# Interleaving three passes of a windowed transformer in larger pieces, normalising P before it is turned, and multiplying with the values as the stationary operand

## The chip, the core and the metric

The kernel runs on one core of one Trainium2 chip. A core has five engines that work side by side, each through its own queue of instructions in order: TensorE (PE; its weight loads are listed as PEld), VectorE (DVE), ScalarE (ACT), GpSimd (POOL) and SyncE (SP), which issues most of the DMA transfers. PE reads two operands from SBUF, a stationary one that is loaded into the array and a moving one that is streamed through it, and writes its results to PSUM. The metric is the time of one execution on the device in microseconds (us), the median of the runs.

## The reference, cut to what matters

The model has four layers, each the product of a mixing branch and a gating branch. Two of the gating branches are complete transformers over the tokens: the first of six layers, 16 heads of 64 and a window of 32; the second of two layers, 8 heads of 64 and a window of 64. Each of their layers computes, for x of 4 x 512 tokens by 128:

```python
qkv = shift(x) @ Wqkv                       # q, k, v by heads of 64
q, k = rotary(l2norm(q) * qs), rotary(l2norm(k) * ks)
sim  = q . k                                # per window: own and previous block of keys
attn = softmax(where(mask, -max, 8 * sim))  # over 2 * window keys
x    = x + concat_heads(attn @ v) @ Wo
x    = x + ((xn @ W1a + b) * gelu(xn @ W1g + b)) @ W2 + b2   # xn: layer norm of shift(x)
```

The change touches these two transformers alone. All of it is in float32, apart from the additive mask, which is bfloat16.

## The kernel before

The kernel computes the layers one after the other. The two transformers (`transformer`, line 707, and the class `_Transformer`, line 1171) fill the stretches from about 1580 to 3410 us and from about 3480 to 3940 us of the profiled execution.

A transformer is run by three passes, which are Python generators: `queries_keys` (line 1268) makes q and k, `attention` (line 1476) everything from the scores to the residual, `feed_forward` (line 1523) the rest. A row is one layer of one of the four sequences of 512 tokens, and a slot is a row's group of eight heads: 6 x 4 rows of two groups are 48 slots in the first transformer, 2 x 4 rows of one group are 8 in the second. In each slot `merge` runs the three passes beside each other, each some slots behind the one before it: a pass gives up control with `yield cost`, and the pass that has done the smallest share of its total (10.3 for queries and keys, `attention_weight`, `feed_forward_weights`) goes on. So these costs decide in which order the products of the three passes stand in PE's queue. The framework puts the instructions of each engine into its queue when the program is built, and an engine works through it in order, waiting on semaphores.

The attention pass works in units: in the first transformer a unit is four heads (of a group's eight) over all 512 tokens, in the second four heads over 256 tokens. There are 96 units in the first (two per slot) and 32 in the second (four per slot). With i the unit at hand, the pass does in each step:

- `scores` (line 1370): two products with the mask and 64 small products (16 in the second) of q and k into one PSUM tile; each has 64 rows of the array and 32 columns (64 in the second). DVE takes the maximum (L1399), subtracts it into P (L1403, two instructions), ACT takes the exponential in place (L1408), DVE sums the rows (L1410) and inverts the sums into r (L1412). In the middle of the products stands the turn of unit i-1.
- `turn` (line 1415): eight transposes of P of unit i-1 by PE (L126, operands `core` and `l_P`), and ACT's copy PT (L1424).
- `turn_back` (line 1465) of unit i-2: its weighted values On, which have the tokens on the partitions, are transposed by PE (L126, `core` and `l_On`; eight transposes, four in the second transformer) and copied by ACT into OT (L1474, two instructions). If it is the second unit of a pair, four products with `Wo` (operands `l_OT` and `l_wo`, 512 columns, 256 in the second) and DVE's addition to the residual (L1513) follow.
- `weigh` (line 1427) of unit i-1: 64 products (16 in the second) in which PT is stationary and the values move; the values are `vo`, where two neighbouring blocks share the partitions, or `ve`, where the pairs begin one block earlier. DVE multiplies the result by r into On (L1454, two instructions of 128x512; in the second transformer one such instruction).
- `values` (line 1331): v of a later unit, copied by ACT into `vo`, and from there by SP's DMAs into `ve`.

A float32 product stands in the trace as two matmul records, each with its own weight load; a transpose is one record. All PSUM tiles come from one ring of four (`S2`), each two banks. POOL adds the squares (L1294) and the halves of the rotation (L1298) of q and k, four of each in a slot. DVE multiplies q and k with the tables (L1295, L1297) and with the inverse lengths (L1321), which come from the products with operands `sqp` and `l_k`. SP issues the DMAs that put q and k into the layout of the scores (`l_qk`, 16 in a slot), those of `ve` and the weights.

Of the kernel before, what the change touches and what calls it, by code (L numbers as in the profile page):

```python
# [16 lines left out]
F32 = mybir.dt.float32  # L17
# [1153 lines left out]
class _Transformer:  # L1171
    def __init__(self, net, pre, heads, window, pools, consts):
# [26 lines left out]
        self.attention_weight = 20.4 if self.split else 25.0  # L1199
# [22 lines left out]
    def part(self, kind, l, gp):  # L1222

        key = kind, l, gp
        if key not in self.weights:
# [8 lines left out]
            else:  # L1234
                t = self.WT.tile([128, 4, 128], F32, name=pre + "_wo", bufs=3)
                nc.sync.dma_start(t, a[pre + "Wo"][l][512 * gp : 512 * (gp + 1)].rearrange("(t p) n -> p t n", p=128))
# [31 lines left out]
    def queries_keys(self, rows):  # L1268
# [3 lines left out]
        for l, b in rows:  # L1272
# [4 lines left out]
            for gp in range(self.GP):  # L1277
# [3 lines left out]
                for i in range(2):  # L1281
# [3 lines left out]
                    for g in range(2):  # L1285
                        p = self.S2()
                        for h in range(2):
# [3 lines left out]
                            yield 0.86  # L1291
# [16 lines left out]
    def unit_length(self, sums, t):  # L1308
# [5 lines left out]
        for g in range(2):  # L1314
            net.mm(p[:, g, :], self.ones, sums[g][:, 0, :])
            yield 0.86
# [14 lines left out]
    def values(self, u):  # L1331
# [8 lines left out]
        for u0 in range(0, n, step):  # L1340
            p = self.S2()
            pv = p.rearrange("p a (b c) -> p (a b) c", c=1024 // self.NB)
            for k in range(u0, u0 + step):
                if self.split:
                    for e in range(2):
                        net.mm(pv[64 * e : 64 * e + 64, k - u0, :], hb[:, 64 * k : 64 * k + 64], w[:, 256 * e : 256 * e + 256])
                    yield 0.45
                else:
                    c = 128 * (n * tp + k)
                    net.mm(pv[:, k - u0, :], hb[:, c : c + 128], w)  # L1350
                    yield 0.86
# [18 lines left out]
    def scores(self, qk, tp, j, last):  # L1370
# [7 lines left out]
        for t in range(T):  # L1378
            if last and t == T // 2:
                yield from self.turn(last)  # L1380
            for g in range(2):
# [13 lines left out]
                yield 0.31  # L1395
        n = 4 * T
# [16 lines left out]
        return P, r  # L1413
# [13 lines left out]
    def weigh(self, u):  # L1427

        net, nc, W, T = self.net, self.nc, self.W, self.T
        PT, r, vo, ve, tp, j = (u[k] for k in ("PT", "r", "vo", "ve", "tp", "j"))  # L1430
        On = self.PP.tile([128, 2 * T, 2, 64], F32, name=self.pre + "_On", bufs=1)
        o = self.S2() if self.split else self.M()
        for i in range(2 * T):
            g = i % 2
            for bl in range(self.NB):
                c = self.NB * (T * tp + i // 2) + bl
                v, k = (vo if c % 2 else ve), c // 2 - tp * self.NU
                for e in range(2):
                    if self.split:
                        rows, d = slice(64 * e, 64 * e + 64), 64 * (2 * g + j)  # L1440
                        net.mm(
                            o[W * bl : W * bl + W, e, 64 * i : 64 * i + 64], PT[rows, i, W * bl : W * bl + W],
                            v[rows, k, d : d + 64],
                        )
                    else:
                        n, d = 2 * i + e, 64 * (4 * g + 2 * j + e)
                        net.mm(
                            o[W * bl : W * bl + W, 64 * n : 64 * n + 64], PT[:, n, W * bl : W * bl + W], v[:, k, d : d + 64]
                        )
            yield 0.3 if self.split else 0.15  # L1450
        rv = r.rearrange("p (n e) -> p n e", e=2)
        if self.split:
            for e in range(2):
                nc.vector.tensor_tensor(  # L1454
                    On[:, :, e, :], o[:, e, :].rearrange("p (n d) -> p n d", d=64),
# [251 lines left out]
```

## Time and profile before

| | |
|---|---|
| three runs | 3961.78, 3963.43 (median) and 3975.84 us |
| the profiled execution | 3955.01 us, of which the span from first to last instruction is 3953.3 us |
| PE | 3577.5 us busy, 90% of the span |
| DVE | 2452.6 us, 62% |
| ACT | 1845.0 us, 47% |
| POOL | 1157.9 us, 29% |
| granted TensorE clock | 0.942 of full speed on the mean of the span |

Busy time is the time in which at least one instruction of the engine is under way. Matmuls overlap, and the mean duration of one record is longer than the distance between the starts of two of them, so that a busy PE is not a PE at its peak. A group of instructions is one source line with one operation, its tiles (output, then inputs, buffer numbers left out) and its shape; most matmuls have the line of the helper that issues them, L122, and transposes L126, so that they are told apart by their tiles. For a matmul, 64*32 is the part of the array that it uses (rows by columns), and 64x64 the moving operand (rows by columns).

### The profile page before, as it was taken

What the parts mean: (1) busy time and instruction counts of PE and PEld (TensorE: products, weight loads), DVE (VectorE), ACT (ScalarE), POOL (GpSimd) and SP (SyncE); (2) the same over time, 40 slices, a digit from 0 to 9 for tenths busy, and PEclk for the clock granted to TensorE, in tenths of its full rate; (3) what the DMA queues carried; (4) which work ended last, traced back from release to release, by engine and by line L of the source; (5) the groups of instructions that cost most, each with busy time, mean ns of one, the idle gap of its engine ahead of it and who ended that gap; (6) DMA issues with size and microseconds to landing.
All of it is one profiled execution on the core that took longest, in us unless ns stands there. A gap on an engine that the chain in (4) does not pass through costs nothing.

```text
span 3953.3 us, 105287 instructions
## 1 busy us (share of the span) xinstructions
PE 3577.5 (90%) x46763; PEld 1880.3 (48%) x46891; DVE 2452.6 (62%) x3429; ACT 1845.0 (47%) x2510; POOL 1157.9 (29%) x994
## 2 busy tenths in 40 slices
PE   7786999899999998889999999999999999778887
PEld 4553455444444443444444554554444445445554
DVE  6674555413353341677777787777777777457774
ACT  3343666523133324454555554555455455535555
POOL 1000444300021112533334343343443343033220
PEclk7677999999699999999999999999999999889998
DMA  1000000001000001434344434334334333413221
GB/s 38 8 26 28 1 1 1 30 0 51 2 1 3 3 1 37 106 86 115 88 96 110 98 91 109 95 91 119 93 83 117 86 80 94 130 37 83 54 56 42
DMA packets 123574, 236.12 MB, mean 60 GB/s; under 512 B 29624, under 2 KB 44128, under 8 KB 117728
## 3 DMA queue, kind: packets, MB, share of 16 engines
q1 hardware_dynamic: 114064, 209.58, 21.7%
q10 hardware_dynamic: 8624, 19.29, 1.5%
q8 instruction: 369, 6.05, 0.6%
q0 software_dynamic: 432, 0.51, 0.1%
q14 instruction: 85, 0.70, 0.1%
HBM read 50.08 MB, written 5.54 MB: 14 GB/s over the span
## 4 chain that ended last, share of the span: by engine, by line
PE 62%; DVE 13%; ACT 12%; issue 6%; DMA 3%; POOL 2%; SPq 1%; DVEq 0%; ACTq 0%; POOLq 0%
PE S L122 39%; PE S L126 5%; PE M L122 5%; PE S L1389 4%; PE o L1094 3%; ACT l_P L581 3%; PE o L614 2%; DVE l_rot L1295 2%; DVE rotp L1297 1%; DMA l_tab<-in_k_rot_l 1%; DVE l_rot L1321 1%; PE S L1008 1%; ACT sqp L1293 1%; ACT l_PT L1424 1%; SPq L1328 1%
## 5 line engine op out<-in xcount | busy, mean ns | idle before, releaser
L1298 POOL TENSOR_TENSOR l_rot<-l_rot,rotp 128x1024 f32<-128x1024 f32 x224 | 528.6, 2362 | 324.7 <-DVE rotp L1297 313.3
L1294 POOL TENSOR_TENSOR sqp<-sqp 128x512 f32<-128x512 f32 x224 | 291.5, 1301 | 956.6 <-ACT sqp L1293 952.0
L122 PE MATMUL S<-hb,l_wqk 128*128 128x512 f32 x896 | 476.8, 622 | 38.1 <-ACT l_PT L1424 10.7
L1293 ACT ACTIVATE sqp<-S 128x1024 f32<-128x1024 f32 x224 | 230.2, 1027 | 305.1 <-PE S L122 304.1
L1321 DVE SCALAR_TENSOR_TENSOR l_rot<-S,l_rot 128x1024 f32<-128x1024 f32 x224 | 264.6, 1219 | 133.8 <-ACT S L1318 110.6
L126 PE MATMUL S<-core,l_P 128*128 128x128 f32 x1856 | 266.9, 288 | 40.1 <-ACT l_P L1408 17.3
L122 PE MATMUL S<-l_KT,l_QT 32*128 32x256 f32 (+7 forms) x1536 | 264.2, 510 | 34.7 <-ACT l_P L1116 14.5
L1295 DVE TENSOR_TENSOR l_rot<-S,l_tab 128x1024 f32<-128x1024 f32 x224 | 271.2, 1211 | 24.6 <-ACT sqp L1293 24.0
L1389 PEld LDWEIGHTS S<-l_qk 64*32 64x32 f32 (+1 forms) x13312 | 178.5, 108 | 217.7 <-issue 211.2
L1116 ACT ACTIVATE l_P<-S 128x1024 f32<-128x1024 f32 x160 | 156.7, 1022 | 252.3 <-PE S L122 251.7
L126 PEld LDWEIGHTS S<-core,l_P 128*128 128x128 f32 x1856 | 213.3, 146 | 128.1 <-issue 39.3
L1297 DVE TENSOR_TENSOR rotp<-S,l_tab 128x1024 f32<-128x1024 f32 x224 | 270.8, 1209 | 1.4 <-POOL l_rot L1298 1.3
L1389 PE MATMUL S<-l_qk 64*32 64x64 f32 (+1 forms) x13312 | 249.5, 230 | 18.8 <-DMA l_qk<-l_rot 1.7
L122 PE MATMUL S<-sqp,l_k 128*128 128x512 f32 x448 | 251.9, 648 | 13.4 <-POOL sqp L1294 6.6
L122 PE MATMUL S<-l_wv,hb 128*64 128x256 f32 (+1 forms) x1600 | 237.2, 400 | 5.5 <-DVE rotp L1297 4.2
L1069 DVE TENSOR_REDUCE l_mx<-S 128x2 f32<-128x768 f32 (+1 forms) x192 | 155.0, 864 | 136.7 <-PE S L1008 136.7
L122 PEld LDWEIGHTS S<-l_ve,l_PT 64*32 64x32 f32 (+1 forms) x6656 | 164.3, 108 | 152.5 <-issue 124.9
L1399 DVE TENSOR_REDUCE mx<-S 128x16 f32<-128x1024 f32 (+1 forms) x128 | 156.3, 1221 | 116.1 <-PE S L1389 112.2
L122 PEld LDWEIGHTS S<-hb,l_wqk 128*128 128x128 f32 x896 | 147.2, 191 | 168.6 <-issue 92.0
L122 PE MATMUL S<-l_OT,l_wo 128*128 128x512 f32 (+1 forms) x512 | 218.9, 543 | 8.3 <-DVE ffu L1551 7.9
L1120 POOL TENSOR_SCALAR_AFFINE_SELECT l_P<-l_P 128x256 f32<-128x256 f32 x256 | 99.4, 406 | 417.0 <-ACT l_P L1116 411.6
L1317 ACT ACTIVATE S<-S,l_tiny 128x1024 f32<-128x1024 f32 x112 | 121.9, 1089 | 198.4 <-PE S L122 180.2
(358 smaller groups left out, 6580.1 us busy)
## 6 DMA issues: line engine op xcount, KB each, us to landing
l_qk<-l_rot SPq DMA_DIRECT2D x896, 128.0 KB
l_ve<-l_vo SPq DMA_DIRECT2D x112, 256.0 KB
l_ve<-l_vo SPq DMA_DIRECT2D x96, 224.0 KB
l_tab<-in_k_rot_l ACTq DMA_DIRECT2D x16, 1024.0 KB
l_wqk<-in_l2Wqkv SPq DMA_DIRECT2D x12, 512.0 KB
l_wv<-in_l2Wqkv SPq DMA_DIRECT2D x12, 256.0 KB
l_wo<-in_l2Wo SPq DMA_DIRECT2D x12, 256.0 KB
l_ve<-l_vo SPq DMA_DIRECT2D x24, 128.0 KB
```

What stands on the lines that cost most here:

```text
L122: self.nc.tensor.matmul(out, lhsT, rhs, start=start, stop=stop)
L126: self.nc.tensor.transpose(out, in_, self.ident[:n, :n])
L1069: nc.vector.tensor_reduce(mxv[:, bs, 2 * m + e, 3 - i], s[u][:, :, c : c + n], axis=AX.X, op=ALU.max)
L1116: nc.scalar.activation(P[u], s[u], AF.Exp, scale=scale)
L1293: nc.scalar.activation(sq, p, AF.Square)
L1294: nc.gpsimd.tensor_tensor(sq[:, 0, :], sq[:, 0, :], sq[:, 1, :], ALU.add)
L1295: nc.vector.tensor_tensor(t[:, g], p, tab[:, 0], ALU.mult)
L1297: nc.vector.tensor_tensor(m, p, tab[:, 1], ALU.mult)
L1298: nc.gpsimd.tensor_tensor(t[:, g], t[:, g], m[:, ::-1, :], ALU.add)
L1321: nc.vector.scalar_tensor_tensor(t[:, g], p[:, g, :].unsqueeze(1).to_broadcast([128, 2, S]), 1e12, t[:, g], ALU.min, ALU.mult)
L1389: net.nc.tensor.matmul(sv[W * bl : W * bl + W, e, t, g, :].rearrange("p (s k) -> p s k", s=2), qk[0][r, g, j, W * c : W * c + W], kw, star ...
L1399: nc.vector.tensor_reduce(mx, flat, axis=AX.X, op=ALU.max)
```

## The change

Five things are edited, all in the two transformers.

1. The weighted values. In `weigh` the values become the stationary operand (64 rows and 64 columns of the array in the first transformer, 128 and 64 in the second) and PT the moving one, of 32 columns (64 in the second). The number of products stays at 64 (16). The result has the head's dimension on the partitions, which is what `Wo` needs: `turn_back` goes, with its transposes, and ACT copies the result into OT with two instructions of 128x512 (one in the second transformer, where there were two of 128x256).
2. The normalisation. As the tokens are no longer on the partitions after `weigh`, P itself is multiplied by r before it is turned, by one POOL instruction of 128x1024 per unit. DVE's multiplications L1454 go.
3. In the first transformer the blocks of even and odd number lie in different halves of PSUM and of the partitions, so that `Wo` is loaded a second time with its two halves of 64 rows exchanged (two more DMAs per load, two buffers of twice the size in place of three), and the product with `Wo` is eight products of 256 columns in place of four of 512.
4. The turn of unit i-1 stands behind all the scores of unit i in place of the middle of them.
5. A pass gives up control less often: after two products of q or k, after both sums of squares, after a whole PSUM tile of values, after half a unit of scores, after half a unit of `weigh`, after two products with `Wo`. The costs are those of the pieces together, and `attention_weight` is 18.6 and 23.0 in place of 20.4 and 25.0.

```diff
-        self.attention_weight = 20.4 if self.split else 25.0
+        self.attention_weight = 18.6 if self.split else 23.0
...
-                t = self.WT.tile([128, 4, 128], F32, name=pre + "_wo", bufs=3)
-                nc.sync.dma_start(t, a[pre + "Wo"][l][512 * gp : 512 * (gp + 1)].rearrange("(t p) n -> p t n", p=128))
+                t = self.WT.tile([128, 2 if self.split else 1, 4, 128], F32, name=pre + "_wo", bufs=2)
+                wo = a[pre + "Wo"][l][512 * gp : 512 * (gp + 1)].rearrange("(t p) n -> p t n", p=128)
+                nc.sync.dma_start(t[:, 0], wo)
+                if self.split:
+                    nc.sync.dma_start(t[0:64, 1], wo[64:128])
+                    nc.sync.dma_start(t[64:128, 1], wo[0:64])
...
                             net.mm(o.rearrange("p (s u k) -> p s u k", s=2, k=W) if i else o, w[:, c : c + 128], hk if i else hb)
-                            yield 0.86
+                        yield 1.72
...
             net.mm(p[:, g, :], self.ones, sums[g][:, 0, :])
-            yield 0.86
+        yield 1.72
...
                         net.mm(pv[64 * e : 64 * e + 64, k - u0, :], hb[:, 64 * k : 64 * k + 64], w[:, 256 * e : 256 * e + 256])
-                    yield 0.45
...
-                    yield 0.86
+            yield 1.8 if self.split else 1.72
...
         for t in range(T):
-            if last and t == T // 2:
-                yield from self.turn(last)
             for g in range(2):
...
-                yield 0.31
+            if t % 2:
+                yield 1.24
...
-        return P, r
+        Pn = P.rearrange("p t g e k -> p (t g e) k")
+        nc.gpsimd.tensor_tensor(Pn, Pn, r.unsqueeze(2).to_broadcast([128, n, 2 * W]), ALU.mult)
+        if last:
+            yield from self.turn(last)
+        return P
...
-                        net.mm(
-                            o[W * bl : W * bl + W, e, 64 * i : 64 * i + 64], PT[rows, i, W * bl : W * bl + W],
-                            v[rows, k, d : d + 64],
-                        )
+                        rows, d, s = slice(64 * e, 64 * e + 64), 64 * (2 * g + j), bl % 2
+                        x = 64 * (e ^ s)
+                        net.mm(ov[x : x + 64, s, i, bl // 2, :], v[rows, k, d : d + 64], PT[rows, i, W * bl : W * bl + W])
...
-            yield 0.3 if self.split else 0.15
-        rv = r.rearrange("p (n e) -> p n e", e=2)
-        if self.split:
-            for e in range(2):
-                nc.vector.tensor_tensor(
-                    On[:, :, e, :], o[:, e, :].rearrange("p (n d) -> p n d", d=64),
-                    rv[:, :, e].unsqueeze(2).to_broadcast([128, 2 * T, 64]), ALU.mult,
-                )
...
-    def turn_back(self, u, OT):
...
-        for i in range(2 * T):
-            net.transpose(t[:, i, :], u["On"][:, i].rearrange("p e d -> p (e d)"))
...
-        for g in range(2):
-            self.nc.scalar.copy(ov[:, u["j"], g], tv[:, g])
+            if i % T == T - 1:
+                yield 1.2 if self.split else 0.3
+        for s in range(2 if self.split else 1):
+            n = 2 * W
+            src = (o[:, s, :] if self.split else o).rearrange("p (t g q) -> p g t q", g=2, q=n)
+            dst = OT[:, s].rearrange("p (g j) (t q) -> p j g t q", j=2, q=n)
+            nc.scalar.copy(dst[:, j], src)
...
-                    for t in range(4):
-                        net.mm(p, wo[:, t, :], OT[:, t, :], t == 0, t == 3)
-                        yield 0.86 if self.split else 0.43
+                    parities = 2 if self.split else 1
+                    pv = p.rearrange("p (x s q) -> p s x q", s=parities, q=W)
+                    for s in range(parities):
+                        for t in range(4):
+                            net.mm(pv[:, s], wo[:, s, t, :], OT[:, s, t, :].rearrange("p (x q) -> p x q", q=W), t == 0, t == 3)
+                            if t % 2:
+                                yield 0.86
```

## The prediction

> **What bounds the kernel now.** I read the busy time by stage first, then the groups, then who waits for whom, then the chain in order of time. The page's totals (PE 90%, DVE 62%) mix stages; by stage (columns: busy time and instructions of PE, PEld, DVE, ACT, POOL, then clock, DMA share, GB/s), the first transformer's steady stretch and the second transformer are:
>
> ```profile
> 1690.00:3390.00 1700.00, 1623.06 (x28182) 843.14 (x28272) 1312.26 (x1452) 867.55 (x988) 650.54 (x398) 1.00 0.40 97
> 3560.00:3954.00 394.00, 337.29 (x2693) 192.30 (x2718) 262.85 (x336) 216.60 (x267) 95.09 (x66) 0.96 0.24 58
> ```
>
> PE is busy for 95% of the first and 86% of the second, DVE for 77% and 67%, POOL for 38% and 24%. The first is bound by PE, the second partly by chains. PE's waits in the first stretch (total, times, longest) are small, and the largest is for an instruction that the change removes:
>
> ```profile
> PE S L122 <- DVE l_On L1454: 18.3, 16, 1.4
> PE S L122 <- ACT l_PT L1424: 14.3, 33, 0.8
> PE S L122 <- DVE rotp L1297: 10.3, 11, 2.0
> PE S L122 <- ACT l_OT L1474: 9.2, 24, 1.3
> ```
>
> What PE's time consists of is seen in the chain in order of time (start, us, what):
>
> ```profile
> 2206.40 0.34 PE S L1389 x16
> 2206.74 1.06 PE S L122 x2
> 2207.80 0.66 PE S L1389 x45
> 2208.45 1.02 PE S L126 x8
> 2209.48 0.67 PE S L1389 x46
> ...
> 2220.94 3.63 PE S L122 x8
> ```
>
> The scores' 64*32 records come in bursts cut by 512-column products and transposes. A burst of 16 takes 0.34 us and one of 46 0.67: 0.011 us a record and 0.16 for the burst. Uncut bursts of 128 run to the next product's start in 1.41 us, so I take 0.010 a record and 0.18 a burst. Eight 512-column records take 3.63 and two alone 1.06, so 0.43 each and 0.20 for the run. Values bursts (128*64) cost 0.15 beside 0.108 a record, from their lengths 4 (0.58) and 12 (1.45). **Every change of the array's division costs PE 0.15 to 0.20 us.**
>
> **The change part by part.** PE is the bound, so its sum comes first.
>
> *Transposes of On*: 96 x 8 + 32 x 4 = 896 go. At (1.02 - 0.20) / 8 = 0.103 us each: -92 us. (Bounds: 0.103 and the group's 100.9 us for 728, 0.139.)
>
> *Fewer cuts.* In the order in which the built program has PE's products, runs with the whole array fall from 605 to 312 in the first transformer, bursts with 32 or 64 columns at 64 rows from 514 to 308, values bursts from 183 to 95; in the second from 105 to 68, 63 to 35 and 42 to 32. First: 293 x 0.20 + 206 x 0.18 + 88 x 0.15 = 109; second: 7 + 5 + 2 = 14. Together -123 us. (The removed transposes' runs are in this count.)
>
> *The weighted sum* keeps 12,288 records in the first transformer. Now each loads 32 columns and streams 64, in eight tiles of the array; after it loads 64 and streams 32, in four. In the second transformer it keeps its shape. No record of before is 64*64 with 32 streamed. The nearest rows are the second transformer's scores (64*64, 128 streamed) and its weighted sum (128*64, 64 streamed), start and duration in us:
>
> ```profile
> 3852.44 0.43 PEld L1389 LDWEIGHTS S<-l_qk 64*64 64x64 f32 x16 [0.42 <-issue]
> 3852.45 0.67 PE L1389 MATMUL S<-l_qk 64*64 64x128 f32 x16
> ...
> 3757.98 0.22 PE L122 MATMUL S<-l_ve,l_PT 128*64 128x64 f32 x1
> 3758.03 0.22 PE L122 MATMUL S<-l_vo,l_PT 128*64 128x64 f32 x1
> 3758.04 0.22 PE L122 MATMUL S<-l_ve,l_PT 128*64 128x64 f32 x1
> 3758.09 0.22 PE L122 MATMUL S<-l_vo,l_PT 128*64 128x64 f32 x1
> 3758.10 0.22 PE L122 MATMUL S<-l_ve,l_PT 128*64 128x64 f32 x1
> ```
>
> One half of the array takes a new 64-column weight every 0.058 us (3757.98, 3758.04, 3758.10). Among the 16 loads of the scores the first four, on four different tiles, start within 0.02 us and the next four 0.055 later, so four tiles load side by side: 0.058 / 4 = 0.0146 us a record. Ends: 0.010 if loads stay hidden (0), 0.0267 if the scores' own pace of 16 in 0.43 us is the loads' (+205 us). I take 0.0146, since the first loads show four at once: 12,288 x 0.0046 = **+57 us**.
>
> [...]
>
> *The product with Wo*: 48 x 8 records of 512 columns become 48 x 16 of 256, the same streaming; the second transformer's 256-column group runs at 22.3 us for 83, 0.27 overlapped, against 0.43 for 512, so between 0 and 48 x 16 x 0.05 = 38 us. Consecutive ones start 0.215 apart, half of 0.43: 0.
>
> PE's work: -92 - 123 + 57 = **-158 us**.
>
> *Waits that go*: DVE l_On -18 and ACT l_OT -9; in the second transformer transposes of On waited 8: **-35 us**. DVE loses 2 x 0.667 per unit, ACT's copies stay; neither was the bound: 0.
>
> *The wait that comes.* PT is copied by ACT (1.02 us) and `weigh` needs it. Before, half the scores, On's transposes and Wo stood between the transposes of P and `weigh` (every unit of the first transformer but two had over 1 us of PE work there); after, in PE's order, 48 of 96 units and 15 of 32 in the second have nothing between. From the last transpose's start to the copy's end before it is 1.32 us at best, 1.69 at the third quarter, 2.44 at the ninth tenth (behind another ACT instruction); PE loses some 1.4 after the 0.11 of streaming. 63 x 1.4 = **+88 us**. What is queued behind: all of PE, so this is paid in full. Ends: 1.2 (+76) and 2.3 (+145).
>
> *P on POOL.* L595 does the same in another layer: 128x1024 in 1.89 us. 128 of them, 242 us, on a POOL that is 38% busy; in the first transformer its share becomes about 50%. In POOL's queue it stands among the rotations (2.36) and sums (1.30); behind it wait the sums that PE's `sqp` products need. PE's cover for those is 2.9 us at the lowest quarter against 2.5 to 3.6 measured from product to sum: +5, ends 0 and 48 x 1.9 = 91. The chain of P grows: r is ready 7.2 us after the scores (middle value), P then some 11; the next scores end 19.4 later. Smallest slack in the first transformer 1.4 us: 0. In the second, units are 8 to 10 us apart and 1.3 to 3.4 short in half of them, 28 us in all, in place of 17 for which its turns waited on P: +15, ends 0 and 28.
>
> *SP*: 24 more DMAs at 0.6 us issue, and Wo's tile now waits for its last use but one; `l_qk` and `ve` queue behind. The chain holds 2.85 us of `l_wo` landing once. 12 loads: ends 0 and 35, I take 0, as q and k are made a slot ahead.
>
> *DVE under POOL*: the copies of `hb` take 0.42 us alone and 1.8 beside POOL; 14% more overlap on 2 per slot is 20 us of a DVE with 23% idle: 0.
>
> Sum: -158 - 35 + 88 + 5 + 15 = **-85 us** on the profiled 3955: 3870. The median of the runs lies 8.4 above the profile: **3878 us**, -2.1%.
>
> **Rivals.**
> *A, the waits stay hidden*: other waits shrink as PE pauses for PT. -158 - 35 = -193: 3770. For it: PE's present waits are 3.5% of the stretch. Against: nothing stands between in PE's order.
> *B, the loads are the bound* (slower): the 64*64 weight loads go two at a time, 0.0267 a record, +205 in place of +57: 3878 + 148 = 4026. It decides from 85 / 12,288 = 0.0069 above 0.0146, at 0.0215 us a record. For it: the scores' 16 loads in 0.43 us; against: the four simultaneous starts.
> *C, the gain goes into waits*: the copy comes at 2.4 us for all 63 units (+57) and POOL's queue delays P or the sums by a rotation (2.36) in a quarter of 128 units (+30 with the slack): 3965, no change. For it: PE's time per unit shrinks by 1 us while the chain grows by 4.
>
> **How the numbers follow.** Forecast (3810 to 3930) 0.55; A (3740 to 3810) 0.2; C (3930 to 3990) 0.13; B (above 3990) 0.12. The median of three runs tells about 0.5%, 20 us, from no change. Faster is the first two and a third of C: 0.8; same 0.08; slower B: 0.12. The range leaves out half of A's best and most of B: 3780 to 3985.
>
> **What would show it.** No l_On group; the weighted sum as 64*64 64x32 with bursts of 64 records at 0.0146 each, near 1.1 us; whole-array runs of two 512-column records rarer; PE waiting on ACT l_PT some 60 times over 1 us; POOL's new group at 1.89 us. Wrong if such a burst takes 1.7 us or more (B), or PE's busy share in the first transformer falls under 90% (C).

## The result: 0.6% slower, and the profile after

The changed kernel takes 3992.9 us on the median (six runs, 3986.8 to 3996.6) against 3965.6 us (six runs, 3960.3 to 3981.9): a ratio of 1.0056, with a 95% interval of 1.004 to 1.0072 (estimated over the runs, and not the quotient of the two medians). The forecast was 3878. The profiled execution took 3996.6 us, its span 3994.8.

Busy time by stage, the first and the second transformer (length, then busy time and instructions of PE, PEld, DVE, ACT and POOL, the clock, DMA share, GB/s). The stretches run from a transformer's first product with `l_wqk` to its last with `ffu`, the kernel before first:

```profile
1582.00:3425.00 1843.00, 1740.07 (x29808) 901.80 (x29902) 1403.37 (x1554) 938.97 (x1066) 711.42 (x435) 1.00 0.40 97
3496.00:3947.00 451.00, 387.98 (x3026) 218.57 (x3056) 309.08 (x389) 243.74 (x297) 125.75 (x84) 0.95 0.25 59
```
```profile
1592.00:3438.00 1846.00, 1667.25 (x29520) 986.44 (x29520) 1325.41 (x1363) 942.42 (x1066) 898.15 (x531) 0.97 0.40 99
3515.00:3988.00 473.00, 372.14 (x2928) 213.55 (x2927) 292.29 (x353) 241.13 (x262) 183.25 (x113) 0.90 0.23 56
```

PE is busy for 73 us less in the first and 16 less in the second, and yet the stages are 3 and 22 us longer. So PE stands idle for longer (length less busy time: 103 to 179 us and 63 to 101 us), and its mean clock fell from 1.00 to 0.97 and from 0.95 to 0.90.

The waits of PE in the first transformer, after (total, times, longest), and then the two longest in the second. The last three rows are the kernel before, l_rot and ffu in the first transformer and P in the second:

```profile
PE S L122 <- ACT l_PT L1431: 61.7, 63, 1.8
PE S L122 <- DMA l_wqk<-in_l2Wqkv: 25.0, 2, 14.0
PE S L122 <- DVE l_rot L1326: 23.1, 11, 4.9
PE S L122 <- DVE ffu L1544: 17.6, 18, 1.0
PE S L126 <- DVE rotp L1302: 13.6, 8, 4.6
...
PE S L126 <- POOL l_P L1417: 55.7, 12, 8.4
PE S L122 <- ACT l_PT L1431: 18.3, 16, 1.5
...
PE S L122 <- DVE l_rot L1321: 12.7, 8, 3.0
PE S L122 <- DVE ffu L1551: 2.7, 1, 2.7
PE S L126 <- ACT l_P L1408: 17.3, 10, 5.4
```

The waits for l_On are gone. Those for l_PT, 80 us in both stages, are the wait that was forecast (before, they were 17.5 us). Three others grew beyond the forecast: the weights of queries and keys (25 us in two waits, none before), l_rot and ffu (41 us; 15 before), and P in the second transformer (55.7 us; 17.3 before).

**The half clock.** PE in order of time around one new pause (start, us, instruction, and in brackets the idle time before it):

```profile
2497.73 2.74 PE L122 MATMUL S<-ffu,l_w 128*128 128x512 f32 x6
2500.31 1.04 PE L126 MATMUL S<-core,l_P 128*128 128x128 f32 x8
2503.11 0.25 PE L122 MATMUL S<-l_PT,l_ve 64*64 64x32 f32 x2 [1.76 <-ACT l_PT L1431]
...
2504.52 3.25 PE L122 MATMUL S<-sqp,l_k 128*128 128x512 f32 x4
...
2507.70 0.25 PE L122 MATMUL S<-l_PT,l_ve 64*64 64x32 f32 x2
...
2508.77 1.52 PE L122 MATMUL S<-l_wv,hb 128*64 128x256 f32 x12
```

PE has finished the transposes at 2501.35 and waits 1.76 us for the copy. The four products with `sqp` that follow take 3.25 us, where four such products take 1.98 at 1836.00 in the same trace: up to 2507.11 they run at half the clock. The 64 records of the weighted sum behind them, 2507.70 to 2508.77, take 1.07 us again.

The trace lists the granted clock in stretches that are multiples of 3.41 us, at 1.0 or 0.5. Counted from the first instruction, as all times here are, one at 0.5 runs from 2503.70 to 2507.11. In the trace after, 84 products of 512 columns are followed by another with the same operands after 0.75 to 1.0 us, and 81 of them lie in a stretch at 0.5; of the 1565 followed after 0.38 to 0.50 us none does. In both transformers the changed kernel has 37 such stretches, 11 before. In 11 of the 24 in its first transformer, the largest piece of PE's idle time in the 3.41 us ahead was a wait for l_PT, in 8 one for l_rot or rotp, in 2 one for l_wqk; in 9 of the 13 in the second, it was a wait for P.

**The sum of PE's time** can then be split for any trace into idle time, the loss by the half clock (half of PE's busy time inside those stretches) and the rest, PE's work at full clock. For both transformers together:

| us | length | idle | loss by half clock | work at full clock |
|---|---|---|---|---|
| before | 2293.9 | 165.5 | 24.7 | 2103.7 |
| after | 2319.4 | 279.4 | 78.8 | 1961.2 |
| difference | +25.5 | +114 | +54 | -142 |

The work fell nearly as forecast (-158). Idle time rose by 114 us where the forecast's waits make +73, and the half clock took another 54 that it did not have. The remaining 16 us of the 41.5 between the two profiled executions lie outside the transformers, where no code is changed.

### The profile page after: what moved, and what is told of

Read it like the earlier page. It is cut to its first block, busy times and chain, and to the rows that moved or that the text cites. A ratio compares the mean times of both kernels' runs of the same rounds, so it can differ in the third digit from the quotient of the medians.

```text
span 3994.8 us, 104509 instructions
## 1 busy us (share of the span) xinstructions
PE 3506.1 (88%) x46379; PEld 1972.1 (49%) x46379; DVE 2360.9 (59%) x3205; ACT 1848.2 (46%) x2478; POOL 1406.7 (35%) x1122
## 5 line engine op out<-in xcount | busy, mean ns | idle before, releaser
L122 PE MATMUL S<-hb,l_wqk 128*128 128x512 f32 x896 | 448.1, 624 | 68.5 <-DMA l_wqk<-in_l2Wqkv 25.0
L1326 DVE SCALAR_TENSOR_TENSOR l_rot<-S,l_rot 128x1024 f32<-128x1024 f32 x224 | 265.3, 1219 | 208.6 <-ACT S L1323 179.4
L122 PE MATMUL S<-l_PT,l_ve 64*64 64x32 f32 (+1 forms) x6656 | 249.0, 225 | 82.3 <-ACT l_PT L1431 75.0
L122 PEld LDWEIGHTS S<-l_PT,l_ve 64*64 64x64 f32 (+1 forms) x6656 | 225.2, 139 | 187.3 <-ACT l_PT L1431 99.1
L1417 POOL TENSOR_TENSOR l_P<-l_P,r 128x1024 f32<-128x1024 f32 x128 | 248.6, 1942 | 161.2 <-DVE r L1415 155.2
L122 PE MATMUL S<-l_KT,l_QT 32*128 32x256 f32 (+7 forms) x1536 | 274.5, 530 | 33.7 <-ACT l_P L1116 14.5
L122 PEld LDWEIGHTS S<-hb,l_wqk 128*128 128x128 f32 x896 | 161.9, 195 | 243.1 <-issue 168.7
L122 PE MATMUL S<-sqp,l_k 128*128 128x512 f32 x448 | 245.6, 672 | 11.3 <-POOL sqp L1299 4.1
L122 PE MATMUL S<-l_PT,l_vo 64*64 64x32 f32 (+1 forms) x6656 | 247.4, 224 | 0.0
L1391 PEld LDWEIGHTS S<-l_qk 64*32 64x32 f32 (+1 forms) x13312 | 166.7, 108 | 122.7 <-issue 117.0
L122 PEld LDWEIGHTS S<-l_PT,l_vo 64*64 64x64 f32 (+1 forms) x6656 | 225.3, 140 | 0.0
L122 PE MATMUL S<-l_wv,hb 128*64 128x256 f32 (+1 forms) x1600 | 218.3, 394 | 7.2 <-ACT l_OT L1465 3.6
```

Of the source, the lines that this page charges most:

```text
L122: self.nc.tensor.matmul(out, lhsT, rhs, start=start, stop=stop)
L1326: nc.vector.scalar_tensor_tensor(t[:, g], p[:, g, :].unsqueeze(1).to_broadcast([128, 2, S]), 1e12, t[:, g], ALU.min, ALU.mult)
L1391: net.nc.tensor.matmul(sv[W * bl : W * bl + W, e, t, g, :].rearrange("p (s k) -> p s k", s=2), qk[0][r, g, j, W * c : W * c + W], kw, star ...
L1417: nc.gpsimd.tensor_tensor(Pn, Pn, r.unsqueeze(2).to_broadcast([128, n, 2 * W]), ALU.mult)
```

## The experiments

Three theories at the start. W: PE's pauses for PT cost their length, and the half clock after them once more. L: the loads at the borders of layers, requested late, cost the gain. N: P, normalised on POOL, comes late, and with it what depends on it or stands behind it on POOL. Two more, P and C, concern the coarse steps (part 5 of the change), and a later one, G, the clock. All kernels, with the split of both transformers' time from their profiles:

| kernel | median, us | ratio to before (95% interval) | idle | half clock | work |
|---|---|---|---|---|---|
| after | 3992.9 | 1.0056 (1.0040 to 1.0072) | 279 | 79 | 1961 |
| coarse steps alone | 3897.4 | 0.9839 (0.9820 to 0.9859) | 159 | 32 | 2040 |
| all but the coarse steps | 4129.7 | 1.0441 (1.0404 to 1.0478) | 307 | 137 | 2019 |
| turn in the middle | 4001.0 | 1.0096 (1.0079 to 1.0114) | 275 | 80 | 1982 |
| turn's cost 3.0 | 3967.0 | 1.0014 (0.9997 to 1.0031) | 259 | 62 | 1964 |
| filled pause | 3984.8 | 1.0065 (1.0047 to 1.0083) | 197 | 43 | 2076 |
| filled with narrow products | 4006.7 | 1.0116 (1.0082 to 1.0150) | 207 | 56 | 2068 |
| early request | 3953.8 | 0.9972 (0.9950 to 0.9993) | 270 | 61 | 1944 |
| P on DVE | 4009.7 | 1.0137 (1.0096 to 1.0179) | 327 | 77 | 1945 |
| early request, costs spread | 3974.2 | 1.0047 (1.0028 to 1.0065) | 265 | 86 | 1955 |
| the same, P on DVE | 3975.7 | 1.0045 (1.0026 to 1.0065) | 274 | 80 | 1959 |
| early request, half the turns in the middle | 3950.8 | 0.9974 (0.9957 to 0.9991) | 265 | 64 | 1956 |
| early request, values ahead | 3888.3 | 0.9814 (0.9786 to 0.9842) | 234 | 63 | 1931 |
| the same, second transformer as before | 3856.4 | 0.9738 (0.9713 to 0.9764) | 166 | 39 | 1984 |
| the same, requests earlier still | 3852.8 | 0.9730 (0.9708 to 0.9753) | 168 | 40 | 1989 |
| coarse steps in the first transformer alone | 3878.7 | 0.9797 (0.9761 to 0.9832) | 163 | 27 | 2023 |

The ratios compare each kernel with runs of the kernel before made beside it, whose medians lie between 3960.4 and 3965.6. So a difference of the medians of two kernels, as the text gives it, can be some 15 us off that of their ratios.

### The coarse steps by themselves, and all but them

The kernel before with part 5 alone:

```diff
                             net.mm(o.rearrange("p (s u k) -> p s u k", s=2, k=W) if i else o, w[:, c : c + 128], hk if i else hb)
-                            yield 0.86
+                        yield 1.72
...
-                yield 0.31
+            if t % 2:
+                yield 1.24
...
-            yield 0.3 if self.split else 0.15
+            if i % T == T - 1:
+                yield 1.2 if self.split else 0.3
```

(and so on for the sums, the values and the product with Wo).

> The kernel before, with one part of the change alone: a pass yields after pairs of products and half units in place of single ones; transposes of On, weighed sum, P on DVE and the place of the transposes of P stay. By the prediction's price of a cut (0.15 to 0.20 us) fewer cuts are worth up to 123 us: theory P (the price holds and the steps cost nothing else) 3850 to 3900. Theory W: coarse steps leave PE without other work at its waits; part of the gain is lost, 3900 to 3950. Theory C (the coarse steps are what makes the change slow): 3965 or above.

3897.4 us: theory P, at the upper end of its range. Work fell by 64 us, idle time by 7, and the half clock took 7 more. So one of the five edits gives 1.6%, and the other four together cost 95 us on top of it.

The opposite, the changed kernel with the single steps of before:

```diff
-                        yield 1.72
+                            yield 0.86
...
-            if t % 2:
-                yield 1.24
+                yield 0.31
```

> The changed kernel with the coarse steps alone undone: a pass yields after single products again (the costs as before). If the price of a cut (0.15 to 0.20 us) holds beside the other parts too, PE has some 60 to 70 us more work, and the time rises to 4040 to 4060. If single steps put more products between the transposes of P and the weighed sum, waits for l_PT (59 us in the first transformer) and half clock (24 stretches) shrink, and the time stays within 20 of the changed kernel's.

4129.7 us, outside both expectations. The price of a cut about holds: work rises by 57 us. The waits for l_PT in the first transformer shrink as expected, from 61.7 to 18.6 us. But others come, and the loss by the half clock rises by 58 us in place of falling. PE's waits in its first transformer:

```profile
PE S L122 <- DMA l_wqk<-in_l2Wqkv: 70.3, 5, 14.7
PE S L122 <- DVE rotp L1302: 30.5, 19, 4.1
PE S L126 <- DVE rotp L1302: 26.3, 16, 1.9
PE S L122 <- ACT l_PT L1431: 18.6, 52, 1.1
```

With single steps, parts 1 to 4 cost 164 us (3965.6 to 4129.7), with coarse ones 95 (3897.4 to 3992.9); by the ratios, 175 and 86. In both cases they save some 80 us of work (2104 to 2019, 2040 to 1961). What follows is about these four parts.

### The pause between the turn and the weighted sum

Part 4 undone, the turn in the middle of the scores again:

```diff
         for t in range(T):
+            if last and t == T // 2:
+                yield from self.turn(last)
...
-        if last:
-            yield from self.turn(last)
         return P
```

> The changed kernel with one part undone: the transposes of P stand in the middle of the scores again; the weighed sum, P on POOL, Wo twice and the coarse steps stay. Theory W (the pauses of PE for PT, each paid with its length and, through the half clock that follows a pause, once more): PE's waits for l_PT in the stretch 1690 to 3390 fall from 59.5 us (61 times) to some 10 to 20, the stretches of half clock in the first transformer from 24 to 15 or fewer, and the time by 50 to 90 us, to 3900 to 3945. Theory L (the loads at the borders of layers, requested late on SP): the borders stay as they are, the time falls by no more than 20, to 3970 or above. Theory N (P normalised on POOL comes late): the transposes now stand earlier, so they wait for P longer; the waits for l_P grow over 59 us and the time rises or stays.

4001.0 us. The waits for l_PT went as theory W has it (61.7 to 11.3 us in the first transformer), the time and the clock did not: 22 stretches of half clock stay in the first transformer, where theory W had 15 or fewer. Idle time is 275 us (279) with other names. PE's waits in the first transformer, and the longest in the second:

```profile
PE S L122 <- DVE rotp L1302: 31.2, 20, 4.4
PE S L122 <- DMA l_wqk<-in_l2Wqkv: 25.3, 2, 16.6
PE S L122 <- DMA l_wv<-in_l2Wqkv: 15.7, 4, 5.0
PE S L126 <- POOL l_P L1419: 14.6, 10, 2.4
...
PE S L126 <- POOL l_P L1419: 67.2, 22, 8.3
```

Turned earlier, P is late more often: 82 us in all, as theory N expects. So with P normalised before the turn, the turn is too early in the middle and leaves a pause at the end.

The same instructions as the changed kernel, with other costs for the planner (`merge`):

```diff
         self.nc.scalar.copy(u["PT"], t)
-        yield 0.9
+        yield 3.0
...
-                yield 1.2 if self.split else 0.3
+                yield 0.15 if self.split else 0.1
```

> The changed kernel, with the same instructions: only the planner is told that the transposes of P cost 3.0 in place of 0.9 and each half of a weighed sum 0.15 in place of 1.2 (the sum of a unit unchanged), so that it puts other passes' products between the transposes and the weighed sum. Theory W: PE's waits for l_PT fall under 25 us, half clock becomes rarer, the time falls by 40 to 90 us, to 3900 to 3950. Theory L: the waits for l_PT fall too, but the time by no more than 20. Theory N: waits for l_P stay at 59 us in the second transformer, the second transformer stays at 473 us and only the first gains.

3967.0 us, 26 below the changed kernel (17 by the ratios) and short of W's range. The waits for l_PT fell to 12 us, those for l_wqk doubled from 25.0 to 49.8, and the idle time fell by 20 us only. Theory N is missed too: the second transformer came to 460 us, where it was to stay at 473.

Four useless products ahead of each weighted sum:

```diff
             ov = o.rearrange("p (i x q) -> p i x q", x=2, q=W)
+        for _ in range(4):
+            net.mm(o[:, 0, :] if self.split else o, self.identb, self.mask[:, 0, :])
```

> The changed kernel with four useless products of 512 bf16 columns (some 0.86 us in all) into the weighed sum's PSUM tile, ahead of the weighed sum; the result is overwritten. They cost 0.86 x 65 = 56 us in the units where PE had other work there, and nothing in the 63 where it waited for PT. If the half clock comes from the pauses (theory W's second half), the stretches of half clock in the first transformer fall from 24 to under 14, and 25 to 40 us come back: the time rises by 15 to 30 us only. If the clock has other causes, they stay at about 24 and the time rises by 50 us or more.

3984.8 us, level with the changed kernel (ratios 1.0065 and 1.0056, their intervals overlap) where 15 to 30 us above it were expected. PE has 115 us more work, and all of it is paid for: idle time falls by 83 us and the loss by half clock by 36; the stretches of half clock in the first transformer fall from 24 to 9. This is the second half of theory W: keep PE at work in the pauses, and the clock comes back.

### The weights at the borders of layers

SP's queue in the changed kernel at the first border of layers (start, us, instruction), and then the same place with the weights requested before the last rearrangement of q and k:

```profile
1847.37 20.45 SPq L1333 DMA_DIRECT2D l_qk<-l_rot  x16
1867.88 0.59 SPq L1229 DMA_DIRECT2D l_wqk<-in_l2Wqkv  x1
```
```profile
1837.22 5.22 SPq L1336 DMA_DIRECT2D l_qk<-l_rot  x8
1842.49 0.59 SPq L1229 DMA_DIRECT2D l_wqk<-in_l2Wqkv  x1
1852.48 5.38 SPq L1336 DMA_DIRECT2D l_qk<-l_rot  x8
```

In the changed kernel the request stands behind 16 DMAs of `l_qk`, which take 20.45 us as they wait for DVE's `l_rot` (L1326; eight that follow each other take 5.22); PE's first product with these weights starts at 1872.1, after 14.0 us of waiting. The kernel with the early request:

```diff
                     before = sums, t
+                k = rows.index((l, b)) * self.GP + gp + 1
+                if k < len(rows) * self.GP:
+                    self.part("qk", rows[k // self.GP][0], k % self.GP)
                 made.append((yield from self.unit_length(*before)))
```

> The changed kernel; only the weights of the next slot's queries and keys are requested before the last rearrangement of this slot's, so that they stand ahead of its DMAs in SP's queue. Theory L (the borders of layers lose because these weights are requested late): PE's waits for l_wqk (25.0 us in the first transformer) and the 10 to 20 us that a border takes more than before go, the time falls by 25 to 60 us, to 3935 to 3970. Theory W: the waits for l_wqk go, but PE then waits at the border for the tables, the rotations or PT, and the time falls by under 15.

3953.8 us, 39 below the changed kernel (33 by the ratios): theory L, in its range. No wait for l_wqk is left in the first transformer. It takes 1801 us in place of 1846: 15 less of idle time, 17 of half clock and 13 of work. The waits for l_PT are much the same (65.3 us, 62 times).

### P on DVE

```diff
-        nc.gpsimd.tensor_tensor(Pn, Pn, r.unsqueeze(2).to_broadcast([128, n, 2 * W]), ALU.mult)
+        nc.vector.tensor_tensor(Pn, Pn, r.unsqueeze(2).to_broadcast([128, n, 2 * W]), ALU.mult)
```

> The changed kernel; only P is normalised on DVE, not on POOL. Theory N (POOL makes P late, and with it the rotations and sums behind it in its queue): the second transformer, 473 us, comes back to 460 or less, waits for l_P and rotp shrink, the time falls by 15 to 40 us. Against it: DVE has some 140 us of work more in a stretch where it is busy 77%, and PE's waits for DVE (rotp, l_rot, ffu: 68 us together) grow, the time stays or rises by up to 30.

4009.7 us, 17 above the changed kernel (32 by the ratios). In the profiled execution, which is the slowest of the four (4029.5), the second transformer gained 6 us only (473.5 to 467.8) and the first lost 35 (1846 to 1881). Two waits grew most in the first, for rotp, products of DVE, from 21 to 39 us, and for the weights:

```profile
PE S L122 <- DMA l_wqk<-in_l2Wqkv: 60.0, 5, 14.4
```

That is 35 us more than the 25.0 of the changed kernel, as much as the whole loss. So taking P off POOL does not win the time back, but as the weights came later in the same run, it does not tell what POOL alone costs in the first transformer; the pair with the early request, next, has the same wait for the weights in both kernels.

### Costs that spread the weighted sum, with and without DVE

```diff
-        yield 0.9
+        yield 3.0
...
             if t % 2:
-                yield 1.24
+                yield 0.7
```

with the early request kept.

> The changed kernel with the early request of the weights, and the planner told 3.0 for the transposes of P and 0.7 for each quarter of the scores, the weighed sum left at 2 x 1.2, so that products of 512 columns stand between the transposes and the weighed sum and inside the weighed sum. If pauses and half clock together cost the change its gain, idle time of PE in both transformers falls from 279 to under 200 us and the half clock's loss from 85 to under 50: 3850 to 3900. If the waits only move (P, the rotations or the sums come late instead), it stays above 3930.

> As the one with the early request and the other costs, and P normalised on DVE. If POOL's place in the chain of P costs the rest, it lies 15 to 40 us below that kernel, in the second transformer above all; if DVE's 140 us more of work count, it lies above it.

3974.2 and 3975.7 us: the waits only moved. Those for l_PT fell from 65.3 to 10.0 us in the first transformer, but those for l_wqk came back with 40.8 us in the other order (39.9 with P on DVE), and the wait for P in the second rose to 73.8. On DVE the second transformer gained 34 us (488 to 454) and the first lost 41, with 29 us more of waits for rotp: theory N holds for the second transformer in this order, and the sum is nil.

### Is it PE's idleness or the array's that costs the clock?

Theory G rests on a wrong zero. The clock's entries were counted from the start of the trace and the products from the first instruction, 10.6 us later, so that stretches of half clock seemed to follow windows in which PE was always busy, with small products. The windows that begin 13.7 and 10.2 us ahead are in truth the one just ahead of the half clock and the slow one itself. This led to narrow filling:

```diff
-            net.mm(o[:, 0, :] if self.split else o, self.identb, self.mask[:, 0, :])
+            net.mm((o[:, 0, :] if self.split else o)[0:32], self.identb[0:32, 0:32], self.mask[0:32, 0, :])
```

> As the kernel with four useless products of 512 bf16 columns ahead of each weighed sum, but on a corner of 32 x 32 of the array in place of 128 x 128: the same streaming time, a sixteenth of the cells at work. Theory G (the clock is granted by how much of the array works, not by whether PE has an instruction): in the stretches of half clock of the changed kernel the two windows of 3.41 us that begin 13.7 us and 10.2 us before them hold under 0.45 of the array's full work; the narrow products add next to nothing to that, so some 20 stretches of half clock stay in the first transformer (9 with the full products) and the time is 25 to 60 us above that of the full products (3985): 4010 to 4045. If only PE's pauses count, both fill kernels have the same clock and time, 3985 within 15.

13 stretches in the first transformer (9 with full products, 24 without filling; G expected 20), and 4006.7 us, 22 above the full products. Neither expectation is met. With both counted from the first instruction, the 18 traces of this case answer the question (both transformers, windows of 3.41 us at full clock, and how often the next window was granted half the clock):

| PE busy in the window | windows | followed by half clock |
|---|---|---|
| under 40% | 351 | 351 |
| 40 to 50% | 129 | 82 |
| 50 to 60% | 251 | 33 |
| over 60% | 10422 | 6 |

In the example above the window from 2500.29 to 2503.70, with the pause of 1.76 us in it, was busy for 48%, and the one from 2503.70 on ran at half clock: a pause of half a window was enough there. So PE's idle time, counted by windows, goes with the clock. Theory G falls: in 2481 of the windows over 60% the whole array was at work for under 45% of the time, and half clock followed 6 of them. Where the 22 us between the two fillings come from stays open: in the transformers it is 15, by the split 13 of half clock and 10 of idle time, less 8 of work.

### Useful work in the pause

Of two units, one has the product with Wo between turn and weighted sum and the other nothing. This kernel (with the early request) puts the first half of the next values there, with five half tiles of `vo` in place of two whole ones and one `w2` in place of two:

```diff
+            early = u and i + 2 < len(units) and u["j"] == 0 and self.split
+            if early:
+                ahead = self.values(units[i + 2])
+                yield from until_none(ahead)
             if last:
                 if last["j"] == 0:
                     OT = self.TP.tile([128, 2, 4, 256] if self.split else [128, 1, 4, 256], F32, name=self.pre + "_OT", bufs=1)
                 yield from self.weigh(last, OT)
-            if u and i + 2 < len(units) and u["j"] == 0:
+            if early:
+                pass
+            elif u and i + 2 < len(units) and u["j"] == 0:
...
-            w2 = WT.tile([128, 3, 128], F32, name=pre + "_w2", bufs=2)
+            w2 = WT.tile([128, 3, 128], F32, name=pre + "_w2", bufs=1)
```

> The changed kernel with the early request of the weights, and in the first transformer the first half of the next unit's values (1.9 us of products) stands between the transposes of P and the weighed sum in the units that have no product with Wo there (vo in half tiles, five of them; one tile less of w2). Theory W: PE's waits for l_PT fall from 65 to under 20 us, idle time in the first transformer from 164 to some 110, half clock's loss stays at 20 to 33; the first transformer takes 1735 to 1765, the kernel 3885 to 3920 (3954 with the early request alone). If the waits only move to another product, it stays above 3935.

3888.3 us, in theory W's range: 65 below the early request alone, and below the kernel before. The first transformer takes 1755 us in place of 1801. Its waits:

```profile
PE S L122 <- DMA l_wqk<-in_l2Wqkv: 29.0, 5, 7.7
PE S L122 <- DMA l_wo<-in_l2Wo: 16.2, 5, 3.8
PE S L122 <- DVE l_rot L1329: 10.4, 7, 3.8
PE S L122 <- ACT l_PT L1438: 9.8, 18, 1.3
```

The wait for l_PT went from 65.3 to 9.8, and idle time fell by 36 us and work by 13; loads are late again (45 us). The half clock did not come back: 16 stretches and 34 us in the first transformer, 16 and 31 with the early request alone. Ten of the 16 now follow windows whose longest wait was for l_wqk or l_wo. Here the pause was closed with work that nothing waits for at once, and the turn stayed where P is ready.

The same units treated in the other way, with the turn back in the middle where no product with Wo follows:

```diff
+            if last and t == T // 2 and self.split and j == 0:
+                yield from self.turn(last)
...
-        if last:
+        if last and not (self.split and j == 0):
             yield from self.turn(last)
```

> The changed kernel with the early request of the weights, and the transposes of P back in the middle of the scores in those units of the first transformer that have no product with Wo behind them; in the others they stay behind the scores. Theory W: waits for l_PT fall under 25 us without the waits for rotp (30 us) that the kernel with all transposes in the middle has: 3890 to 3930. If the place of the transposes in the middle delays P's chain, rotp and the rotations again, it stays above 3940.

3950.8 us, no gain on the early request: waits for l_PT 15 us, for l_wqk 33, l_wo 18, ffu 17, rotp 11. An earlier turn did not pay here, even in half of the units.

### The second transformer

Coarse steps in the first transformer alone, the second as in the kernel before (a second copy of the class):

```diff
-            t = _Transformer(self, pre, heads, window, pools, consts)
+            t = (_Transformer if pre == "l2" else _SecondTransformer)(self, pre, heads, window, pools, consts)
```

> The kernel before with the coarse steps in the first transformer alone; the second is as before. With coarse steps in both, the first took 1768 (before: 1843) and the second 462 us (before: 451). If the steps act on each stage by itself, 3897 - 12 = 3885, between 3875 and 3895. If the second transformer's 462 was chance, 3897.

> The kernel with the values between the transposes of P and the weighed sum, but the second transformer as in the kernel before. The second transformer took 474 us there and 448 to 451 in the kernels that leave it as before: 3888 - 25 = 3863, between 3850 and 3875. If the two stages share something that this leaves out, it stays above 3880.

3878.7 and 3856.4 us, both in range: 19 and 32 us below the same kernels with both transformers changed. The second transformer takes 448 and 449 us; with coarse steps alone it takes 462, with the whole change 473.5. So by themselves the coarse steps cost this stage 12 us of the 23 that the whole change costs. The parts do not add up, though: with single steps beside the other four parts it takes 488 us, 15 more than with coarse ones. Single steps are better there in the order of the kernel before alone, and the shares of the parts in the 23 us stay open.

### Requests earlier still

```diff
                         if before:
+                            k = rows.index((l, b)) * self.GP + gp + 1
+                            if k < len(rows) * self.GP:
+                                self.part("qk", rows[k // self.GP][0], k % self.GP)
                             made.append((yield from self.unit_length(*before)))
...
                 if i % of_slot == 0:
+                    if self.split:
+                        self.part("o", u["l"], u["gp"])
```

(in place of the request further down).

> As the kernel with the values ahead and the second transformer as before; the weights of the next slot's queries and keys are requested half a slot earlier still, and Wo at the start of its slot. If the waits for l_wqk (29 us) and l_wo (16 us) are a loss of their own, they go and the time falls by 25 to 45, to 3815 to 3840. If PE then waits at the borders for the tables or the rotations, it falls by under 10.

> As the kernel with early requests, and the weighed sum yields after each quarter. Cost: two more cuts per unit, 192 x 0.17 = 33 us of PE. If the half clock follows from long runs of small products, stretches of half clock in the first transformer fall from some 16 to under 8 and 25 to 35 us come back: within 12 of the kernel with halves. If the length of the runs has nothing to do with it, it is 25 to 40 us slower.

3852.8 us, 3.6 below the kernel without, as the second expectation has it (under 10): the waits for l_wqk and l_wo went, and one for the weights of the values came, 23.3 us in 4 waits. The kernel with quarters (edit: `if i % 2: yield 0.6`) took 3864.0 us, ratio 0.9746 (0.9708 to 0.9784). The planner put its quarters together again: in both kernels all 96 weighted sums of the first transformer are uncut bursts of 128 records. So it repeats its neighbour, shows that two such builds lie within 0.3%, and leaves its question untested.

The kernel with the early requests is faster than both kernels, by 2.7% than the one before.

## Why the prediction was wrong, by its steps

- **PE's work**: -158 forecast, -142 measured. The weighted sum's loads were weighed rightly: 64 records from 2507.70 to 2508.77 are 1.07 us. In the first transformer 90 bursts of 64 records take 1.065 us on the median and 51 of 128 take 1.998, which is 0.0146 us a record, as forecast, and 0.13 a burst (0.15 to 0.20 forecast for a change of division). Rival B (0.0267, 4026) falls. Its pace, that of the 16 loads of the scores in 0.43 us, is not the pace here. The price of a cut about held too (64 us of work for the coarse steps by themselves, 57 beside the other parts, where 60 to 70 were expected).
- **The wait for PT**: +88 forecast, 80 us measured (61.7 and 18.3), of which the kernel before had 17.5 already, so that 62 came on top. The mechanism was right and the size a little high. What was missing is that a pause can cost more than its length, as the next step shows.
- **The half clock**: not in the sum, +54. This is the step that failed most. The forecast quoted a clock column that fell to 0.96 where PE had pauses, and gave it no price. 63 pauses were forecast, each of 1.4 us. Of the windows of 3.41 us in which PE was busy for 40 to 50%, 82 of 129 were followed by one at half clock, and of those with 50 to 60%, 33 of 251. The filled pause (24 to 9 stretches) shows that PE's idle time is the cause. Only 11 of the 24 stretches of the first transformer follow mainly a wait for PT; the others follow waits that the forecast had at little or nothing, and with those for PT nearly closed but these left (the turn in the middle, 22 stretches) the clock stayed low.
- **SP**: 0 forecast, ends 0 and 35. "As q and k are made a slot ahead" was the cover that failed: the weights for making them stood in the same queue, behind DMAs that wait for DVE's `l_rot`. The early request gave 39 us (33 by the ratios). That is the second failed step. Why the request stands further back in the changed kernel's queue than in the one with coarse steps, which has no such wait, was not tried.
- **P on POOL**: +20 forecast, of which 15 for the second transformer. The wait for P there rose from 17.3 to 55.7 us, the stage by 23. This was mis-sized. The coarse steps, which the forecast counted as a gain of 14 there, cost the stage 12 us by themselves but save 15 beside the other parts. P on DVE gained 6 us of it in the order of the changed kernel and 34 in the order with spread costs.
- **Fewer waits elsewhere**, rival A, fell. Rival C was nearest in time (3965), by the idea that the gain goes into waits, but not by its mechanism: the copy of PT was not later than forecast, and POOL's queue in the first transformer cost next to nothing (3.7 us of waits for l_P). By its number alone, 3992.9 would fall to B (above 3990), whose mechanism the bursts rule out.

In sum, 110 us lie between the forecast's -85 and the +25 measured in the transformers: some 16 of work, 41 of idle time and 54 of clock.

## What to carry to other kernels

When a change takes work from a bound engine and adds a pause at the same place, price the pause by the window of the clock that it falls into (3.41 us here), not by its length alone, and look for work without a deadline to put there; moving the waiting instruction earlier only moved the wait here (l_PT in the first transformer from 61.7 to 11.3 us, l_P in both from 59 to 82). Try each edit of a bundle by itself: here one of five was worth 1.6% by itself and the others hid it. And follow every request of weights through its queue at the border of a layer, where what stands ahead of it may wait for something else (20.45 us here).

## What the runs showed of the hardware

A window of 3.41 us in which PE is busy for under 40% is followed by one at half clock in 351 of 351 cases, one with over 60% in 6 of 10422. The clock's entries fit the products only if both are counted from the same instruction (81 of 84 slow products and none of 1565 others); counted 10.6 us apart they point to the wrong cause. Products with weights of 64 rows by 64 columns, four to the array, follow each other at 0.0146 us a record (64 in 1.065 us and 128 in 1.998), a quarter of the 0.058 us between two records with 128 rows by 64 columns on one half of the array in the kernel before (3757.98, 3758.04 and 3758.10).
